# A hybrid block of delta-rule attention, SSD and two quantised FFNs: the last level of a block inverse done by 64x64 quarters, one decay read from an exponential, and a new instruction order

## The chip, the cores and the metric

The kernel runs on one core of a Trainium2 chip. The metric is the device time of one execution in microseconds; lower is better. Every run below is of the same inputs.

## The reference

A batch of 32 sequences of 256 tokens, 128 features each, goes through four residual layers: gated delta-rule attention, a feed-forward layer with int32 weights scaled by 1/127, an SSD (state-space) layer, and the same feed-forward layer again. Each begins with a layer norm.

```python
x = x + attn(_layernorm(x))   # below
x = x + ffn(_layernorm(x))    # silu(x wg^T) * (x wu^T), then wd^T; 128 -> 384 -> 128
x = x + ssd(_layernorm(x))
x = x + ffn(_layernorm(x))
```

The attention keeps a 128x128 state per sequence and updates it token by token:

```python
def step(S, ins):
    q_t, k_t, v_t, a_t, b_t, g_t = ins
    kkT = k_t[:, :, None] * k_t[:, None, :]
    trans = a_t[:, :, None] * (I - b_t[:, :, None] * kkT)
    vkT = v_t[:, :, None] * k_t[:, None, :]
    S = jnp.einsum('bij,bjk->bik', S, trans) + b_t[:, :, None] * vkT
    o = jnp.einsum('bc,bcd->bd', q_t, S) * g_t
    return (S, o)
```

The SSD layer projects to z, x, B, C and dt, applies a causal convolution of 4 taps and a silu to x, B and C, and computes a decayed, causal sum over the tokens with 4 heads of 64 channels. With `dA = dt * A` and its running sum `cs`, the weight of token j in the output of token i is `(C_i . B_j) * exp(cs_i - cs_j) * dt_j`, for j up to i. Then come a gate by silu(z), an RMS norm and an output projection.

## The kernel before

**Units and tiles.** Two sequences, 512 tokens, make a unit; there are 16 units. A unit's activations are NT = 4 tiles of 128 tokens by 128 features, kept as one 128 x 512 tile. Everything is float32, save for the three bfloat16 pieces that some SSD sums are cut into. A float32 matmul is two passes of TensorE, a transpose one.

**Attention as chunks.** A sequence is two chunks of 128 tokens. Inside a chunk the recurrence is a triangular system: with `neg` (lines 726 to 740) holding the negative decayed products of the keys (`diag` is its four diagonal 128x128 blocks), the kernel needs the inverse of (I - diag) of each. It is built in two stages.
- The 16x16 blocks on the diagonal, by substitution. Eight DMAs (`blocks`, line 748) write the blocks to DRAM and eight more (`rows`, 757) read them back, each broadcast over its 16 partitions. Then 15 pairs of small VectorE instructions, `step` and `u` (764 to 771), make the inverses of all blocks at once, and one GpSimd multiply (`x`, 774) sets them on the diagonal of the 128 x 512 tile `x`.
- Three levels (`LEVELS` = 16, 32, 64; lines 781 to 795) merge pairs of blocks of size d into blocks of 2d. For each of the four tiles: transpose x (`pt`), copy to SBUF (`t`, ScalarE), multiply by `diag` (`p1`), copy (`pm`, ScalarE), multiply by x (`p3`). Then one VectorE `copy_predicated` of 128 x 512 puts those parts of `p3` into `x` that a mask of this level, `m_d`, names. The inverse serves the rest of attention (`wq`, `z`, `po`, `py`).

**SSD.** `pz` gives z and dt, a short chain on VectorE turns dt into `dt` and GpSimd into `dA`. From `dA` come two things. First, `pe`: a matmul with the constant `gt` (ones where the row's token comes after the column's) sums what remains to the end of the first chunk, and one with `le` sums what has passed in the second; `ee` is the exponential of both, `f0 = dt * ee[:, 0]` on GpSimd, and `xe = x * f0` weighs the first chunk's tokens for the sum that goes on to the second chunk (`pf`). Secondly, `cs` (a matmul with 32 columns of weights, `grid`): its sums are cut into three bfloat16 pieces (`cut`), go through DRAM in six DMAs (`cuts`, `sums_s`, `sums_t`) and come back in two row layouts, from which one matmul, `pl`, gives the exponents of all pairs of tokens of a tile. The exponential is taken in place in PSUM; times C.B it is `sm`, and `sy` are four matmuls with it.

**The planner.** No instruction is issued where the code stands. Every call records an operation in a `Planner` (from line 140), with an engine, a modelled busy time, a modelled `late` (what passes after the engine is free until the result can be used) and what it depends on. `run` then goes through the recorded operations as a list scheduler and emits one fixed order per engine: PE (TensorE), VectorE, ScalarE, GpSimd and SP (SyncE, which issues the DMAs). An operation's key is the due time of its unit (`at`: unit number x `period`, with the last units drawn together by `LAST`), plus the distance from the longest chain, plus an offset `STAGE` for its layer. `HOP` is the cost of passing to another engine, `SLACK` the cost of reusing a buffer, `SWITCH` the price put on a change of ScalarE's table, `EARLY` how soon a PSUM bank may be taken before it is needed, `window` how many units may be open. The model's DMA takes 450 ns on SP and its `late` after that, however many are under way. At run time each engine goes through its list strictly in order and waits by semaphores.

**Lines.** As all operations are recorded, the profile gives one line for each kind: L211 is every matmul, L221 every transpose, L231 every activation and L229 every copy on ScalarE, L245 every VectorE instruction, L262 GpSimd, L270 the DMAs. Tiles are told apart by their names, with a letter for the layer: `_a` attention, `_f` and `_h` the two feed-forward layers, `_s` SSD. `p_a` is both `p1` and `p3`, `pt_a` the transposes of the levels, `sm_s`, `sy_ps_s` and `pf_s` those of SSD, `pd_a` the transposes of the decays, with 4 columns of result partitions.

Of the kernel before, what the change touches and what calls it, by code (L numbers as in the profile page):

```python
# [12 lines left out]
BF16 = mybir.dt.bfloat16  # L13
# [4 lines left out]
P = 128  # L18
SEQS = 2
# [126 lines left out]
class Planner:  # L146
# [4 lines left out]
    SLOTS = {"ps": 8, "m": 56, "l": 10, "t": 12, "s": 64, "d": 6, "g": 6, "b": 3, "e": 4}  # L151
    SWITCH = 38400.0
    HOP, SLACK = 100.0, 0.0
    STAGE = (100.0, 0.0, 1700.0, 4100.0)
    EARLY = 2800.0
    SPARE = {"ps": 0.5, "m": 3, "l": 0.5, "t": 1, "s": 2, "d": 0.5, "g": 0.5, "b": 0.5, "e": 0.5}
    LAST = 0.29
    HALF = "be"
    SIZES = {"ps": 512, "m": 512, "l": 1024, "t": 64, "s": 32, "d": 512, "g": 8192, "b": 384, "e": 12288}

# [16 lines left out]
    def add(self, eng, busy, late, emit, outs, ins, table=None, after=(), lock=False):  # L177
        op = Op()
        op.eng, op.busy, op.late, op.emit, op.table, op.lock = eng, busy, late, emit, table, lock
        op.unit, op.n, op.stage = self.unit, len(self.ops), self.stage  # L180
        op.preds, op.succs, op.bufs = {p.n: p for p in after}, [], []
        for v, write in [(v, False) for v in ins] + [(v, True) for v in outs]:
# [35 lines left out]

    def transpose(self, out, in_, ident):
        def emit():  # L220
            self.tc.nc.tensor.transpose(real(out), real(in_), real(ident))  # L221

        self.add("PE", 109, 165, emit, [out], [in_, ident])

# [41 lines left out]

    def dma(self, out, in_, late=3500, queue="SP"):
        def emit():
            engine = self.tc.nc.sync if queue == "SP" else self.tc.nc.scalar
            engine.dma_start(out=real(out), in_=real(in_))  # L270

        self.add(queue, 450, late, emit, [out], [in_])

# [22 lines left out]
    def run(self):  # L296
# [18 lines left out]
        free = dict.fromkeys(engines, 0.0)  # L315
        lock = 0.0
        cands = {e: [] for e in engines}
        slots = {k: [[0.0, i] for i in range(n)] for k, n in self.SLOTS.items()}
# [5 lines left out]
        while len(order) < len(ops):  # L324
            best = None
            for e in engines:
                rest = []
                for op in cands[e]:
                    if op.unit > oldest + self.window:
                        continue  # L330
                    t = max(free[e], op.ready, lock if op.lock else 0.0)
                    ok = True
                    for b in op.bufs:
# [77 lines left out]
def hybrid_block(ctx: ExitStack, tc: tile.TileContext, ins: dict, out: bass.AP):  # L411
# [68 lines left out]
    mask_x = []  # L480
    for d in LEVELS:
        nb = P // (2 * d)
# [150 lines left out]
    def attention(g, x):  # L633
# [26 lines left out]
        copy(row_sb.part(first), pd.part(first))  # L660
        pl.dma(row[0, :].rearrange("(j p) -> j p", p=P), row_sb.part(first), late=3000)
        dec = big([P, SEQS, 2 * P], f"dec_{n}")
        pl.dma(dec.rearrange("p s t -> p (s t)"), row.via(lambda r: r[0, :].partition_broadcast(P)), late=6000)

# [81 lines left out]
        for b in range(NBLK):  # L746
            at = slice(b * BLOCK, (b + 1) * BLOCK)
            pl.dma(
                blocks[0, :].rearrange("(b t j i) -> b j t i", b=NBLK, t=NT, i=BLOCK)[b, :, :, :],
                diag[:, :, at].part(at), late=5000,  # L750
            )
        rows_n = pl.buf("l", [P, NT, BLOCK, BLOCK], f"rows_{n}")
        spread = rows_n.rearrange("p t j i -> p (t j i)")
        for b in range(NBLK):
# [4 lines left out]
                blocks[0, b * size : (b + 1) * size].via(lambda ap: ap.partition_broadcast(BLOCK)),  # L759
                late=6000,  # L760
            )
# [18 lines left out]

        for lv, d in enumerate(LEVELS):
            pt = bank([P, NT, P], f"pt_{n}_{d}")
# [74 lines left out]
    def ssd(g, x):  # L857
# [55 lines left out]
        for i in range(3):  # L913
            pl.dma(
                rows_d[0, :].rearrange("(q i j t) -> i q j t", i=3, j=NT, t=P)[i, :, :, :],
                cut[:, i, :], late=3500,
            )
        s_rows, t_rows = sums_s[g % 2], sums_t[g % 2]
        pl.dma(
            s_rows.part(slice(0, parts)).rearrange("p j t -> p (j t)"),  # L920
            rows_d[0, :].rearrange("(k t) -> k t", t=TOK), late=4000,
        )
        for o in range(2):
            pl.dma(
                t_rows.part(slice(parts + 3 * o, parts + 3 * o + 3)).rearrange("p h j t -> p h (j t)"),
                rows_d[0, :].rearrange("(o h i t) -> o i h t", o=2, h=NH, i=3)[o, :, :, :], late=4000,
            )
# [22 lines left out]
        for s in range(SEQS):  # L950
# [24 lines left out]
            for c in range(2):  # L975
# [97 lines left out]
```

## Time and profile before

| What | us |
|---|---|
| Three runs | 884.88, 884.69, 880.66 |
| Median | 884.69 |
| The profiled execution | 883.38 |
| Its span, first to last instruction | 881.7 |
| PE busy from 200 to 800 us of the span | 594.5 of 600 |
| VectorE busy in that stretch | 485.9 |
| ScalarE busy in that stretch | 441.8 |
| GpSimd busy in that stretch | 218.6 |
| DMA: bytes over the span | 25.3 MB, 29 GB/s |

The profile's engines are PE (TensorE's matmuls), PEld (its weight loads, which overlap PE), DVE (VectorE), ACT (ScalarE), POOL (GpSimd) and SP (the DMA issues). A row of a group reads: line, engine, operation, output tile <- input tiles, shape, count | busy time in us, mean duration in ns | idle time of the engine just before those instructions, and what ended most of it. The slices are 40 equal parts of the span, each digit a tenth of the slice; PEclk is the clock that TensorE was granted, in tenths of full speed. Matmuls are pipelined, so their mean duration is a latency, and several overlap.

### The profile page before, as it was taken

The page shows a single profiled execution, that of the slowest core. Times are in us where ns is not written, and L with a number is a line of the kernel's source. Part 1 is how long each engine was busy: PE and PEld are TensorE (multiplying, and loading weights), DVE is VectorE, ACT ScalarE, POOL GpSimd, SP SyncE. Part 2 cuts the span into 40 slices and gives each one's busy share as a digit, 9 for nine tenths or more (in the row PEclk, how much of TensorE's full clock was granted, in tenths as well). Part 3 has the DMA queues.
Part 4 walks back from the last instruction along what each step waited for, and adds up shares of the span by engine and source line. Part 5 has one row for each costly group of instructions (what it writes and reads, how often), then busy time and mean ns, then how long its engine had stood idle before and what let it go on. Part 6 is the DMA issues. An engine that isn't in the chain of part 4 may idle for free.

```text
span 881.7 us, 15941 instructions
## 1 busy us (share of the span) xinstructions
PE 841.8 (95%) x5145; PEld 654.9 (74%) x5145; DVE 696.4 (79%) x2298; ACT 620.5 (70%) x1385; POOL 347.5 (39%) x581
## 2 busy tenths in 40 slices
PE   4967999999999999999999999999999999999997
PEld 3646877778777788777778877778788787585785
DVE  5676599987989889787988879789967647779972
ACT  4842568584977868685876868588685674789862
POOL 7992234342433525252442535234432022142630
PEclk9987999999999999999999999999999999999999
DMA  6220110001101020110102011011110000000001
GB/s 156 64 73 2 38 26 26 21 1 27 40 25 38 4 54 14 30 37 27 40 1 54 13 29 38 27 41 27 36 30 17 1 1 17 0 13 4 20 1 37
DMA packets 42147, 25.34 MB, mean 29 GB/s; under 512 B 18448, under 2 KB 37840, under 8 KB 42064
## 3 DMA queue, kind: packets, MB, share of 16 engines
q1 hardware_dynamic: 40768, 24.00, 10.5%
q8 instruction: 41, 0.67, 0.3%
q10 hardware_dynamic: 1296, 0.33, 0.2%
q14 instruction: 42, 0.34, 0.1%
HBM read 19.16 MB, written 5.14 MB: 28 GB/s over the span
## 4 chain that ended last, share of the span: by engine, by line
PE 78%; DVE 10%; ACT 6%; POOL 3%; DMA 1%; issue 1%; DVEq 0%; ACTq 0%; SPq 0%
PE p_a L211 9%; PE sy_ps_s L211 6%; PE pc_s L211 5%; PE fg_f L211 5%; PE fu_f L211 5%; PE fy_f L211 4%; PE fg_h L211 4%; PE fu_h L211 4%; PE fy_h L211 4%; PE so_s L211 3%; PE pt_a L221 2%; PE pz_s L211 2%; PE wq_a L211 2%; PE po_a L211 2%; ACT L231 2%; DVE cy_s L245 2%
## 5 line engine op out<-in xcount | busy, mean ns | idle before, releaser
L245 DVE SCALAR_TENSOR_TENSOR cy_s<-pc_s,cw,cy_s 128x510 f32<-128x510 f32 (+2 forms) x192 | 134.2, 734 | 1.4 <-ACT cy_s L231 1.0
L231 ACT ACT_TABLE_LOAD x72 | 92.4, 1283 | 8.9 <-DMA bab<-in_L_attn_a_bb_dram 7.6
L211 PEld LDWEIGHTS fy_h<-wdT,hT_h 128*128 128x128 f32 x384 | 61.8, 191 | 24.5 <-issue 22.5
L211 PE MATMUL fy_f<-wdT,hT_f 128*128 128x128 f32 x384 | 73.7, 275 | 0.0
L211 PEld LDWEIGHTS fy_f<-wdT,hT_f 128*128 128x128 f32 x384 | 61.1, 191 | 13.5 <-issue 12.4
L211 PE MATMUL fy_h<-wdT,hT_h 128*128 128x128 f32 x384 | 68.9, 275 | 0.0
L245 DVE TENSOR_TENSOR step_a<-rows_a,u_a 128x60 f32<-128x60 f32 (+14 forms) x240 | 59.4, 247 | 5.8 <-issue 1.5
L211 PE MATMUL pc_s<-xT_s,w_xbc 128*128 128x512 f32 x128 | 63.8, 596 | 0.1
L245 DVE TENSOR_TENSOR u_a<-u_a,step_a 128x60 f32<-128x60 f32 (+14 forms) x240 | 58.8, 245 | 4.0
L211 PE MATMUL sy_ps_s<-xd_s,sm_s 128*128 128x64 f32 x512 | 60.4, 273 | 1.0 <-DVE sm_s L245 1.0
L211 PEld LDWEIGHTS sy_ps_s<-xd_s,sm_s 128*128 128x128 f32 x512 | 59.3, 192 | 1.6 <-DVE sm_s L245 1.2
L231 ACT ACTIVATE cy_s<-pc_s,cb,cw 128x512 f32<-128x512 f32 x64 | 48.3, 774 | 13.3 <-PE pc_s L211 13.1
L211 PEld LDWEIGHTS p_a<-t_a,neg_a 128*128 128x128 f32 x384 | 50.0, 198 | 8.3 <-issue 4.3
L211 PE MATMUL p_a<-t_a,neg_a 128*128 128x128 f32 x384 | 54.3, 284 | 1.4 <-ACT t_a L229 1.4
L262 POOL TENSOR_TENSOR sy_s<-sy_s,yo_s 128x256 f32<-128x256 f32 x32 | 23.6, 756 | 81.0 <-DVE yo_s L245 67.8
L245 DVE COPY_PREDICATED x_a<-m,p_a 128x512 f32<-128x512 int32 x48 | 34.9, 728 | 25.6 <-PE p_a L211 25.4
L211 PE MATMUL p_a<-x_a,pm_a 128*128 128x128 f32 x384 | 54.0, 279 | 0.9 <-ACT pm_a L229 0.9
L211 PEld LDWEIGHTS p_a<-x_a,pm_a 128*128 128x128 f32 x384 | 50.2, 194 | 4.9 <-ACT pm_a L229 1.8
L229 ACT COPY pm_a<-p_a 128x512 f32<-128x512 f32 x48 | 28.1, 584 | 35.3 <-PE p_a L211 35.2
L211 PE MATMUL fg_h<-xT_h,wgT 128*128 128x512 f32 x96 | 48.9, 599 | 0.9 <-ACT fth_h L231 0.6
L245 DVE TENSOR_TENSOR hT_f<-fth_f,fu_f 128x512 f32<-128x512 f32 x48 | 32.8, 683 | 20.8 <-PE fu_f L211 17.9
L211 PE MATMUL fu_f<-xT_f,wuT 128*128 128x512 f32 x96 | 48.6, 592 | 0.0
(214 smaller groups left out, 2364.5 us busy)
## 6 DMA issues: line engine op xcount, KB each, us to landing
rows_a<-blocks_a SPq DMA_DIRECT2D x128, 64.0 KB
x<-in_L_attn_a_x_dram SPq DMA_DIRECT2D x16, 256.0 KB
dec_a<-row_a SPq DMA_DIRECT2D x16, 256.0 KB
out_dram<-x SPq DMA_DIRECT2D x16, 256.0 KB
blocks_a<-neg_a SPq DMA_DIRECT2D x128, 4.0 KB
cuts_s<-cut_s SPq DMA_DIRECT2D x48, 8.0 KB
sums_t<-cuts_s SPq DMA_DIRECT2D x32, 12.0 KB
sums_s<-cuts_s SPq DMA_DIRECT2D x16, 24.0 KB
```

The source lines that it names most:

```text
L211: self.tc.nc.tensor.matmul(real(out), lhsT=real(lhsT), rhs=real(rhs), start=start, stop=stop)
L221: self.tc.nc.tensor.transpose(real(out), real(in_), real(ident))
L229: self.tc.nc.scalar.copy(real(out), real(in_))
L231: self.tc.nc.scalar.activation(real(out), real(in_), func, bias=real(bias), scale=real(scale), **kw)
L245: getattr(self.tc.nc.vector, name)(real(out), *map(real, args), **{k: real(v) for k, v in kw.items()})
L262: getattr(self.tc.nc.gpsimd, name)(real(out), *map(real, args), **{k: real(v) for k, v in kw.items()})
```

## The change

It has three parts.

**The last level by quarters.** When the two 64x64 blocks on the diagonal of x are inverted, only the upper right 64x64 quarter of each tile is still to be found. The loop runs over `LEVELS[:-1]`, and the level d = 64 is written out with `lo` = 0 to 63 and `hi` = 64 to 127: four transposes of the upper left quarter (64x64), a ScalarE copy `t` of 64 x 256, four matmuls `p1` of 64x64 whose result lies in partitions 64 to 127, a copy `pm` of 64 x 256, four matmuls `p3` of 64x64 whose result lies in partitions 0 to 63, and a ScalarE copy of it into x. VectorE's `copy_predicated` of this level and the mask `m_64` go.

**The decay to a chunk's end.** `gt` and its matmul go. The last column of the exponential `ps` of the first chunk already holds the decay from each token to the chunk's end, so `f0` is now a VectorE multiply of 128 x 4 that reads it from PSUM, once per sequence (two per unit), and `xe` follows it. `ee` keeps its second half only.

**The order.** The planner's model of a DMA gets a transfer time (bytes / `RATE`, at least 150 ns), transfers that pass one after the other, and at most `LANES` = 8 in flight; the `late` values are smaller; and the constants of the list scheduler are others. The list of operations is not touched by this, only their order on each engine. `transpose` gets a modelled cost.

```diff
@@ Planner
-    SWITCH = 38400.0
-    HOP, SLACK = 100.0, 0.0
-    STAGE = (100.0, 0.0, 1700.0, 4100.0)
-    EARLY = 2800.0
+    SWITCH = 22500.0
+    HOP, SLACK = 50.0, 110.0
+    STAGE = (-700.0, -600.0, 24500.0, -12600.0)
+    EARLY = 1800.0
-    LAST = 0.29
+    LAST = 0.15
+    RATE = 270.0
+    LANES = 8
...
-    def transpose(self, out, in_, ident):
+    def transpose(self, out, in_, ident, cost=109):
...
-    def dma(self, out, in_, late=3500, queue="SP"):
+    def dma(self, out, in_, late=2300, queue="SP"):
...
-        self.add(queue, 450, late, emit, [out], [in_])
+        v = out if isinstance(out, View) and out.buf.kind not in "dge" else in_
+        half = v.buf.kind in self.HALF or v.buf.dtype == BF16
+        size = (v.lanes[1] - v.lanes[0]) * _count(v) * (2 if half else 4)
+        moves = max(150.0, size / self.RATE)
+        op = self.add(queue, 450, late + moves - 450, emit, [out], [in_])
+        op.moves, op.first = moves, late
@@ Planner.run
+                    if op.moves and len(landed) >= self.LANES:
+                        t = max(t, landed[-self.LANES])
...
+            if op.moves:
+                moved = max(moved, t + op.first - 900) + op.moves
+                op.done = moved + 900
+                landed.append(op.done)
@@ hybrid_block
-    pl = Planner(tc, pools, period=16400.0, window=6)
+    pl = Planner(tc, pools, period=28300.0, window=6)
...
-    le, gt = pl.const([P, P], "le"), pl.const([P, P], "gt")
+    le = pl.const([P, P], "le")
...
-    pool("memset", gt, 1.0)
-    select(gt, ALU.is_gt, 0, [[-1, P]], 1)
...
-    for d in LEVELS:
+    for d in LEVELS[:-1]:
@@ attention: late of the DMAs row 3000 -> 1100, dec 6000 -> 2400, blocks 5000 -> 1400, rows 6000 -> 2100
...
-        for lv, d in enumerate(LEVELS):
+        for lv, d in enumerate(LEVELS[:-1]):
...
+        d = LEVELS[-1]
+        lo, hi = slice(0, d), slice(d, P)
+        pt = bank([P, NT, d], f"pt_{n}_{d}").part(lo)
+        for j in range(NT):
+            pl.transpose(pt[:, j, :], xi_f[:, j, lo].part(lo), ident[:, lo].part(lo), cost=58)
+        t = big([P, NT, d], f"t_{n}_{d}").part(lo)
+        copy(t, pt)
+        p1 = bank([P, NT, d], f"p1_{n}_{d}").part(hi)
+        for j in range(NT):
+            matmul(p1[:, j, :], diag[:, j, hi].part(lo), t[:, j, :], True, True)
+        pm = big([P, NT, d], f"pm_{n}_{d}").part(hi)
+        copy(pm, p1)
+        p3 = bank([P, NT, d], f"p3_{n}_{d}").part(lo)
+        for j in range(NT):
+            matmul(p3[:, j, :], pm[:, j, :], xi_f[:, j, hi].part(hi), True, True)
+        copy(xi_f[:, :, hi].part(lo), p3)
@@ ssd: late of the DMAs cuts 3500 -> 1700, sums 4000 -> 1600
-        pe = bank([P, 2, SEQS, NH], f"pe_{n}")
-        matmul(pe[:, 0], gt, dA[:, 0::2, :], True, True)
-        matmul(pe[:, 1], le, dA[:, 1::2, :], True, True)
-        ee = small_([P, 2, SEQS, NH], f"ee_{n}")
+        pe = bank([P, SEQS, NH], f"pe_{n}")
+        matmul(pe, le, dA[:, 1::2, :], True, True)
+        ee = small_([P, SEQS, NH], f"ee_{n}")
         act(ee, pe, AF.Exp)
         f0 = small_([P, SEQS, NH], f"f0_{n}")
-        pool("tensor_tensor", f0, dt[:, 0::2, :], ee[:, 0], ALU.mult, cost=285)
...
-            pool("tensor_tensor", xe, xt[:, 0], f0[:, s, :, None].to_broadcast([P, NH, HD]), ALU.mult)
...
                 act(ps, ps, AF.Exp)
+                if c == 0:
+                    vec("tensor_tensor", f0[:, s, :], dt[:, j, :], ps[:, :, P - 1], ALU.mult)
+                    pool("tensor_tensor", xe, xt[:, 0], f0[:, s, :, None].to_broadcast([P, NH, HD]), ALU.mult)
...
-            vec("tensor_tensor", yo, pf, ee[:, 1, s, :, None].to_broadcast([P, NH, HD]), ALU.mult)
+            vec("tensor_tensor", yo, pf, ee[:, s, :, None].to_broadcast([P, NH, HD]), ALU.mult)
```

More of the change, by code (lines that the diff above doesn't have):

```diff
@@ L181, in add @@
         op.preds, op.succs, op.bufs = {p.n: p for p in after}, [], []
+        op.moves = 0.0
         for v, write in [(v, False) for v in ins] + [(v, True) for v in outs]:
@@ L217, in matmul @@
         self.add("PE", busy, 165, emit, [out], [lhsT, rhs], after=after)
-    def transpose(self, out, in_, ident):
+    def transpose(self, out, in_, ident, cost=109):
         def emit():
             self.tc.nc.tensor.transpose(real(out), real(in_), real(ident))
-        self.add("PE", 109, 165, emit, [out], [in_, ident])
+        self.add("PE", cost, 165, emit, [out], [in_, ident])
     def act(self, out, in_, func, bias=0.0, scale=1.0, accum=None):
@@ L316, in run @@
         lock = 0.0
+        moved, landed = 0.0, []
         cands = {e: [] for e in engines}
@@ L660, in attention @@
         copy(row_sb.part(first), pd.part(first))
-        pl.dma(row[0, :].rearrange("(j p) -> j p", p=P), row_sb.part(first), late=3000)
+        pl.dma(row[0, :].rearrange("(j p) -> j p", p=P), row_sb.part(first), late=1100)
         dec = big([P, SEQS, 2 * P], f"dec_{n}")
-        pl.dma(dec.rearrange("p s t -> p (s t)"), row.via(lambda r: r[0, :].partition_broadcast(P)), late=6000)
+        pl.dma(dec.rearrange("p s t -> p (s t)"), row.via(lambda r: r[0, :].partition_broadcast(P)), late=2400)
         sq = big([P, NT, P], f"sq_{n}")
@@ L749, in attention @@
                 blocks[0, :].rearrange("(b t j i) -> b j t i", b=NBLK, t=NT, i=BLOCK)[b, :, :, :],
-                diag[:, :, at].part(at), late=5000,
+                diag[:, :, at].part(at), late=1400,
             )
@@ L759, in attention @@
                 blocks[0, b * size : (b + 1) * size].via(lambda ap: ap.partition_broadcast(BLOCK)),
-                late=6000,
+                late=2100,
             )
@@ L915, in ssd @@
                 rows_d[0, :].rearrange("(q i j t) -> i q j t", i=3, j=NT, t=P)[i, :, :, :],
-                cut[:, i, :], late=3500,
+                cut[:, i, :], late=1700,
             )
@@ L920, in ssd @@
             s_rows.part(slice(0, parts)).rearrange("p j t -> p (j t)"),
-            rows_d[0, :].rearrange("(k t) -> k t", t=TOK), late=4000,
+            rows_d[0, :].rearrange("(k t) -> k t", t=TOK), late=1600,
         )
@@ L925, in ssd @@
                 t_rows.part(slice(parts + 3 * o, parts + 3 * o + 3)).rearrange("p h j t -> p h (j t)"),
-                rows_d[0, :].rearrange("(o h i t) -> o i h t", o=2, h=NH, i=3)[o, :, :, :], late=4000,
+                rows_d[0, :].rearrange("(o h i t) -> o i h t", o=2, h=NH, i=3)[o, :, :, :], late=1600,
             )
```

## The prediction

> **What bounds the kernel.** I read the page's busy shares, slices and chain of waits first, then the busy time by stage, then the groups of instructions by shape, and at last single instructions on the timeline.
>
> ```profile
> PE 841.8 (95%) x5145; PEld 654.9 (74%) x5145; DVE 696.4 (79%) x2298; ACT 620.5 (70%) x1385; POOL 347.5 (39%) x581
> PE   4967999999999999999999999999999999999997
> PEclk9987999999999999999999999999999999999999
> PE 78%; DVE 10%; ACT 6%; POOL 3%; DMA 1%; issue 1%; DVEq 0%; ACTq 0%; SPq 0%
> ```
>
> TensorE is busy 95% of the span and carries 78% of the chain that ended last. The four weak slices at the left are its start, where the granted clock dips too. The stages tell it in numbers (columns: window, its length, then busy time of PE, PEld, DVE, ACT, POOL with counts, then clock, DMA share, GB/s):
>
> ```profile
> 0.00:22.00 22.00, 9.92 (x44) 7.33 (x45) 12.26 (x70) 10.24 (x28) 15.96 (x48) 1.00 0.61 157
> 44.00:66.00 22.00, 14.95 (x52) 8.87 (x52) 16.84 (x43) 9.97 (x24) 20.91 (x35) 0.84 0.27 72
> 66.00:88.00 22.00, 16.75 (x95) 14.49 (x95) 15.21 (x58) 6.15 (x12) 4.58 (x6) 0.77 0.01 4
> 200.00:800.00 600.00, 594.52 (x3709) 466.85 (x3707) 485.89 (x1602) 441.79 (x973) 218.59 (x353) 1.00 0.10 25
> 860.00:882.00 22.00, 17.17 (x87) 11.36 (x85) 6.36 (x10) 5.70 (x11) 1.01 (x1) 0.97 0.13 37
> ```
>
> From 200 to 800 us PE idles 5.5 us in 600: there only less PE work can shorten the time, and DVE (486 of 600) and ACT (442) are worth nothing by themselves. Before 88 us PE idles about 25 us, with POOL full from 44 to 66 us (20.91 of 22); at the end it idles some 5 us. So the change is priced as PE work taken away, idle time at the start, and waits that a new order may put into the 99% full middle.
>
> ```profile
> L211 PE MATMUL p_a<-t_a,neg_a 128*128 128x128 f32 x384 | 54.3, 284 | 1.4 <-ACT t_a L229 1.4
> L211 PE MATMUL p_a<-x_a,pm_a 128*128 128x128 f32 x384 | 54.0, 279 | 0.9 <-ACT pm_a L229 0.9
> L221 PE MATMUL pt_a<-ident,x_a 128*128 128x128 f32 x192 | 31.9, 280 | 3.7 <-DVE x_a L245 3.7
> L211 PE MATMUL pe_s<-dA_s,gt 128*128 128x8 f32 x32 | 4.6, 216 | 0.0
> L245 DVE COPY_PREDICATED x_a<-m,p_a 128x512 f32<-128x512 int32 x48 | 34.9, 728 | 25.6 <-PE p_a L211 25.4
> L229 ACT COPY w_a<-wq_a 128x256 f32<-128x256 f32 x16 | 6.0, 372 | 29.9 <-PE wq_a L211 29.8 <-DVE pr_a L245 0.2
> ```
>
> The mean of a matmul (284 ns) is latency; what it takes from PE is the distance to the next start. In the trace a float32 matmul is two passes, each 430 ns for 512 columns, 217 for 256 and 112 for 128; a 128-column transpose is one pass of 109.
>
> **Part 1, the last level by quarters: PE.** Two 128x128 matmul groups of four per unit become two groups of four of 64x64: 16 units x 8 x 2 = 256 passes of 112 ns, 28.7 us. No 64-column pass of this form is in the trace; from 430, 217 and 112 I estimate 57 ns, 14.6 us. That would save 14.1 us, if a 64x64 matmul sits in the queue like any other. The only float32 matmuls here that don't use the whole array suggest that it doesn't: `cs_s`, a tile 32 columns wide (PE rows, then a PEld row):
>
> ```profile
> 168.49 0.39 PE L211 MATMUL fy_f<-wdT,hT_f 128*128 128x128 f32 x2
> 168.81 0.41 PE L211 MATMUL cs_s<-le,grid_s 128*32 128x128 f32 x2
> 169.14 0.71 PE L211 MATMUL so_s<-w_out,gT_s 128*128 128x128 f32 x4
> 169.14 0.52 PEld L211 LDWEIGHTS so_s<-w_out,gT_s 128*128 128x128 f32 x4 [0.20 <-issue]
> ```
>
> The second `fy_f` pass starts at 168.60, `cs_s` at 168.81 (205 ns later where 112 is usual); its second pass starts at 168.94, the next weights load only at 169.14 after 0.20 us of idle for which no releaser is shown, and that matmul 107 ns later (308 ns from the `cs_s` pass, where I would expect 57 for a 64-column pass). All 16 visits look the same. A visit to another tile size so costs 93 + 251 = 344 ns beyond the passes. In the new PE order the 64x64 matmuls come in 18 + 19 visits (a few groups are split by full-size work): 37 x 0.344 = 12.7 us. Net -1.4 us; ends -14.1 (no visit cost) and -1.4.
>
> The transposes: 64 of 109 ns become 64 of about 58: -3.3 us. Do they pay the visit? The nearest row is the transpose `pd_a`, also into a narrow tile (4 columns): its neighbours stand 109 ns away on both sides, no gap. I take -3.3; with the gap, 21 visits x 0.344 = 7.2, it is +3.9.
>
> [...]
>
> **Part 1, elsewhere.** DVE loses 16 x 728 ns = 11.6 us of copies; ACT gains 16 copies of 128x256 or less (372 ns, 6.0 us) and its 32 other copies shrink from 583 to about 372 (-6.8). Both ends lie behind PE, so I cost them at 0. One level's chain of hops also shortens by 0.2 + 0.2 + 0.35 us; PE work covers it in the middle.
>
> **Part 2, decay from the exponentials.** Sixteen matmuls against `gt` go. The two of `pe_s` in a unit start 142 ns apart in all (31 + 111): 16 x 0.142 = -2.3 us of PE. POOL loses 16 x 204 ns; DVE gains 32 multiplies of 128x4, by the row `z_s` (152 ns) 4.9 us; the net DVE change is -6.8 us. `f_s` was ready early and now waits for the cuts, two DMA trips (7 us measured from the last cut to `pl`) and the exponential; behind that DVE multiply queues `sm_s`, which needs the same exponential anyway, and behind `xe` on POOL (614 ns) queues y's last addition. `pf` waits for `xe` 0.15 + 0.61 us after the exponential, and has `sy` matmuls (8 x 224 ns) between: 0. Without that cover it is 32 x 0.77 = 25 us, which is why I looked at the order: PE has 2.5 us of work from `pl` to `sy` and 3 to 5 from `pf` on.
>
> **Part 3, the order.** The instruction order is fixed in the program, so I added the PE work (by the distances above) that stands between an instruction and the one that depends on it.
> - From `kk1` to the first transpose of the same unit: 57 us in mid-run before, 26 to 27 after. That stretch has to hold `neg`, 16 SP transfers (7.3 us of issue, their landing 2), 30 small DVE steps, and `x_a` on POOL (1.29 us). Before it took 30.0 (first unit), 38 (middle), 26.2 us (last). DVE has 22.4 to 26.0 us of work placed there after, plus 1.6 for `x_a` and hops: 24.0 to 27.6 against 26.5. Mean excess I take as 0.2 us, x 16 = +3; ends 0 and 1 us x 16 = +16.
> - Cuts to `pl`: 25 before, 7 to 10 after, need 7. Hops within a level: 2.6 to 3.5 before, 0.9 to 1.1 after, need 0.84 (163 ns of matmul, 30, the 585 ns copy, 60). Covered: 0; if not, 144 hops x 0.1 = 14, the same size as the loop's bad end.
> - Start: in the first unit the transpose `pt_16` came at 63.7 us with 36.4 us of PE work ahead; after, 25.4. From it to `pt_64` took 14.1 us with 4.9 of work inside; after, 11.0 inside. If `x_a` came at the same time, PE would lose 11.0 - 6.1 = 4.9 us; if it comes e earlier, 4.9 - e. POOL, full to 62 us, has about 10 us less ahead of that `x_a` (fewer later units' front work, no `gt` or `m_64` masks), and DVE's steps waited 3.7 us behind POOL's casts. I take e = 8: -3 us; ends e = 13 (all of both) -8, and e = 0 +5.
> - Table loads on ACT 72 to 66 (1283 ns each): -7.7 us, behind PE, 0. SP has 436 transfers as before. The end: 16.6 us of PE work instead of 19.0 follow the last unit's `so`, a chain of hops bounds it: 0.
>
> **Sum.** PE work -1.4 - 3.3 - 2.3 = -7.0; start -3; loop +3. The profiled execution took 883.4 us (span 881.7), 1.3 below the median 884.7: 883.4 - 7.0 = 876.4. I forecast 876.
>
> **Rivals.**
> - A, *every visit drains, transposes too, and the order gives nothing*: -1.4 + 3.9 - 2.3 = +0.2, so 883.6. For it: `cs_s`, 16 of 16. Against: `pd_a`.
> - B, *no visit cost*: a 64x64 matmul with its own row group is not a 32-column tile. -14.1 - 3.3 - 2.3 - 3 + 3 = -19.7, so 863.7. Against: the only row that exists.
> - C, *the DVE loop becomes the bound*: place, the DVE queue between `neg` and `x_a`; price, about 1 us per unit and 16 us in all; it decides once that stretch takes over 26.5 us. -7.0 - 3 + 16 = +6, so 889.4. For it: 38 us measured in the middle before, though DVE had other work in that time; and DVE already bounds 800 to 840 us. Against: DVE is 79% busy and gets 6.8 us less.
>
> **Numbers.** 0.5% (4.4 us) is about what a measurement of this kernel can tell from no change: faster is below 880.3, slower above 889.1. Chances: the forecast 0.45 (own range 869 to 881), A 0.20 (880 to 886), B 0.13, C 0.22 (886 to 895). The forecast gives 0.43 to faster and 0.02 to same; A 0.18 same, 0.02 faster; B all faster; C 0.02 same and 0.20 slower. Together 0.58, 0.22, 0.20. The range from B's side (861) to C's middle (890) holds 8 in 10.
>
> **What would show it.** Passes of 64x64 near 57 ns and a gap of 0.2 us at both ends of a group say part 1 is right; gaps around `pt` say A, none at all B. The middle's windows should keep PE over 98.5% busy; idle before `pt_16` with `x_a` or DVE steps as releaser says C. The unit-0 `pt_16` should start near 56 us. `pf` waiting on `xe`, or `pl` on the sums, would break part 2's zero. The prediction is wrong if PE busy time does not fall by about 7 us, or if idle in 200 to 800 us exceeds 10.

## The result and the profile after

The changed kernel takes 897.71 us (median of 4 runs, 895.58 to 899.65), against 884.4 for the kernel before in the same job: a ratio of 1.0136, 95% interval 1.0095 to 1.0178. It is slower by 13 us, where 8 us faster was forecast; the range ended at 890. The profiled execution took 899.65 us and has a span of 897.8 us, 16.1 more than before; it lies 2 us above the median, the one before 1 us below it.

The page's busy shares, slices, clock and chain of waits of the changed kernel:

```profile
PE 856.1 (95%) x5113; PEld 646.8 (72%) x5113; DVE 669.4 (75%) x2314; ACT 606.8 (68%) x1395; POOL 349.6 (39%) x559
PE   5689999999999999999999999999999999899897
PEclk9889999999999999999999999999999999989689
PE 69%; ACT 10%; DVE 10%; POOL 5%; issue 2%; DMA 2%; SPq 2%; DVEq 0%; ACTq 0%; POOLq 0%
```

DVE and ACT are busy for 27 and 14 us less (7 and 8.5 were counted; of DVE's, 11.6 are the copies and 17.7 the small steps `step` and `u`, which are as many as before but took less time each, 209 and 210 ns on the mean for 247 and 245; the decay's new multiplies add 4.8), but PE is busy for 14 us *more* with fewer instructions: busy time here also holds passes at a lowered clock and the changes of tile size (13.1 us behind 740 us and 17.4 us in all, worked out below). The second new thing is on the right: the clock falls to 0.6 in a slice near 840 us, where before it was full. By stages (window, length, then busy PE, PEld, DVE, ACT, POOL, clock, DMA share, GB/s), first the kernel before, then the changed one, each from 740 us to its end:

```profile
740.00:881.70 141.70, 133.33 (x769) 97.51 (x767) 103.69 (x303) 99.21 (x208) 45.52 (x73) 1.00 0.05 14
```

```profile
44.00:66.00 22.00, 20.52 (x104) 14.62 (x103) 19.24 (x68) 15.06 (x45) 18.19 (x32) 0.86 0.15 44
66.00:88.00 22.00, 20.36 (x147) 16.41 (x145) 17.55 (x67) 11.69 (x33) 8.88 (x13) 1.00 0.21 51
200.00:800.00 600.00, 589.85 (x3616) 448.53 (x3615) 451.90 (x1561) 420.83 (x956) 212.00 (x328) 0.99 0.09 24
740.00:897.80 157.80, 143.97 (x739) 106.23 (x737) 105.59 (x315) 97.01 (x207) 45.58 (x68) 0.91 0.04 11
```

The start is better filled (20.5 and 20.4 us of PE in windows that had 15.0 and 16.8). But from 740 us on the changed kernel needs 157.8 us where the old one needed 141.7, with fewer PE instructions left (739 against 769).

Busy time misleads here, so I counted starts: each PE pass at its full-speed length (430, 217, 112, 109 ns as in the prediction, 57 or 58 for 64 columns) is *work*; what passes beyond it until the next start is *loss*, be it a wait, a change of tile size or a lowered clock; the time before the first pass and after the last counts as loss too. The two profiled executions then differ so:

| us | before | after | difference |
|---|---|---|---|
| PE work | 811.9 | 792.3 | -19.6 |
| Loss up to 132 us | 41.9 | 37.2 | -4.7 |
| Loss from 132 to 740 us | 14.1 | 33.6 | +19.5 |
| Loss from 740 us to the end | 13.8 | 34.7 | +20.9 |
| Span | 881.7 | 897.8 | +16.1 |

**The middle** is above all the price of the 64x64 tiles. One visit on the PE timeline of the changed kernel (start, length, then the group):

```profile
373.15 0.94 PE L214 MATMUL sy_ps_s<-xd_s,sm_s 128*128 128x64 f32 x7
374.03 0.68 PE L214 MATMUL p_a<-x_a,pm_a 64*64 64x64 f32 x8
374.63 0.77 PE L214 MATMUL sy_ps_s<-xd_s,sm_s 128*128 128x64 f32 x5
```

The seventh `sy` pass starts at 373.82 (112 ns apart), the first 64x64 pass only 205 ns later; they follow each other at 58 ns, the first after 106; the last starts at 374.48, the next `sy` 148 ns later (58 would do) and the one after that 160 (112 would do). Over the visits that have no wait beside them a matmul visit loses 318 ns (36 of 37) and a transpose visit 269 ns (19 of 21). That is 11.8 + 5.6 = 17.4 us, of which 13.2 (27 and 17 visits) fall into the middle; the other 6 there are scattered waits for copies and activations of ScalarE. The groups' rows show the same passes without it:

```profile
L214 PE MATMUL p_a<-x_a,pm_a 64*64 64x64 f32 x128 | 11.4, 225 | 0.0
L214 PE MATMUL p_a<-t_a,neg_a 64*64 64x64 f32 x128 | 11.2, 225 | 0.1
L224 PE MATMUL pt_a<-ident,x_a 64*64 64x64 f32 x64 | 7.5, 224 | 1.5 <-DVE u_a L248 1.5
L224 PE MATMUL pd_a<-ident,ab_a 128*4 128x128 f32 x16 | 4.4, 273 | 0.1
```

No column says what a visit costs: "idle before" is nearly zero, since the gap is counted to nobody.

**The end** is waits and the clock. The longest wait, on the timeline of the changed kernel:

```profile
781.44 1.28 ACT L234 ACT_TABLE_LOAD   x1
781.45 1.03 PE L214 MATMUL pl_s<-sums_t,sums_s 93*128 93x512 bf16 x4
782.86 2.03 ACT L234 ACTIVATE pl_s<-pl_s 128x512 f32<-128x512 f32 x4
784.01 0.73 DVE L248 SCALAR_TENSOR_TENSOR cy_s<-pc_s,cw,cy_s 128x508 f32<-128x508 f32 x1
784.73 0.68 DVE L248 SCALAR_TENSOR_TENSOR sm_s<-pl_s,cb_s 128x512 f32<-128x512 f32 x1
785.55 0.63 PE L214 MATMUL sy_ps_s<-xd_s,sm_s 128*128 128x64 f32 x4 [3.07 <-POOL xe_s L265]
```

`sy` of unit 12 stands in PE's order right behind `pl`. It has to wait for a table load, the exponential and `sm`, which queues behind a convolution step on DVE. (The row names POOL's `xe`, but the first `sm` ends at 785.41, 0.14 us before `sy` starts.) The next work in PE's list is `sy` itself, so PE stands. The windows after it:

```profile
780.00:790.00 10.00, 6.93 (x43) 5.65 (x43) 9.16 (x20) 8.73 (x20) 6.09 (x8) 0.88 0.01 2
790.00:800.00 10.00, 9.86 (x48) 8.24 (x48) 7.47 (x26) 6.20 (x17) 2.62 (x6) 0.78 0.00 0
830.00:840.00 10.00, 7.70 (x40) 6.20 (x38) 8.22 (x18) 9.16 (x20) 6.37 (x9) 0.77 0.04 9
840.00:850.00 10.00, 10.00 (x48) 9.64 (x49) 4.23 (x15) 1.24 (x3) 2.33 (x3) 0.55 0.00 0
```

A window with PE 7 to 8 us busy is followed by one with PE full and a mean clock of 0.78 or 0.55: part of the passes run at half speed (from 835.41 to 849.06 us the granted clock is 0.50, and 128-column passes start 213 ns apart where 112 is usual). Behind 740 us the half clock costs 13.1 us (before: none).

### The profile page after: what moved, and what is told of

Its sections match the earlier page's. It is cut to its first block, busy times and chain, and to the rows that moved or that the text cites. A ratio compares the mean times of both kernels' runs of the same rounds, so it can differ in the third digit from the quotient of the medians.

```text
span 897.8 us, 15836 instructions
## 1 busy us (share of the span) xinstructions
PE 856.1 (95%) x5113; PEld 646.8 (72%) x5113; DVE 669.4 (75%) x2314; ACT 606.8 (68%) x1395; POOL 349.6 (39%) x559
## 4 chain that ended last, share of the span: by engine, by line
PE 69%; ACT 10%; DVE 10%; POOL 5%; issue 2%; DMA 2%; SPq 2%; DVEq 0%; ACTq 0%; POOLq 0%
PE p_a L214 7%; PE sy_ps_s L214 5%; PE fu_h L214 4%; PE fy_f L214 4%; PE fy_h L214 4%; PE fg_h L214 4%; PE fu_f L214 4%; PE pc_s L214 3%; PE fg_f L214 3%; PE so_s L214 2%; PE wq_a L214 2%; ACT L234 2%; PE po_a L214 2%; PE pt_a L224 2%; PE pf_s L214 2%
## 5 line engine op out<-in xcount | busy, mean ns | idle before, releaser
L248 DVE TENSOR_TENSOR step_a<-rows_a,u_a 128x4 f32<-128x4 f32 (+14 forms) x240 | 49.5, 209 | 20.7 <-DMA rows_a<-blocks_a 9.0
L232 ACT COPY t_a<-pt_a 128x512 f32<-128x512 f32 (+1 forms) x48 | 24.4, 512 | 56.7 <-PE pt_a L224 56.5
L234 ACT ACTIVATE cy_s<-pc_s,cb,cw 128x512 f32<-128x512 f32 x64 | 48.5, 780 | 17.7 <-PE pc_s L214 17.6
L265 POOL TENSOR_TENSOR x_a<-u_a,blk 128x512 f32<-128x512 f32 x16 | 20.4, 1274 | 91.8 <-DVE u_a L248 36.5
L248 DVE TENSOR_TENSOR u_a<-u_a,step_a 128x4 f32<-128x4 f32 (+14 forms) x240 | 49.7, 210 | 3.5
L214 PEld LDWEIGHTS p_a<-t_a,neg_a 128*128 128x128 f32 (+1 forms) x384 | 42.1, 172 | 11.6 <-ACT t_a L232 4.0
L265 POOL TENSOR_TENSOR xd_s<-xt_s,dt_s 128x512 f32<-128x512 f32 x32 | 32.9, 1043 | 43.5 <-ACT xt_s L232 38.4
L214 PEld LDWEIGHTS p_a<-x_a,pm_a 128*128 128x128 f32 (+1 forms) x384 | 41.8, 172 | 9.7 <-ACT pm_a L232 4.4
L214 PE MATMUL p_a<-t_a,neg_a 128*128 128x128 f32 (+1 forms) x384 | 48.4, 260 | 0.1
L214 PE MATMUL fg_f<-xT_f,wgT 128*128 128x512 f32 x96 | 47.7, 600 | 0.9 <-ACT fth_f L234 0.9
L214 PE MATMUL p_a<-x_a,pm_a 128*128 128x128 f32 (+1 forms) x384 | 48.0, 261 | 0.3 <-ACT pm_a L232 0.3
```

Of the source, the lines that this page charges most:

```text
L214: self.tc.nc.tensor.matmul(real(out), lhsT=real(lhsT), rhs=real(rhs), start=start, stop=stop)
L232: self.tc.nc.scalar.copy(real(out), real(in_))
L234: self.tc.nc.scalar.activation(real(out), real(in_), func, bias=real(bias), scale=real(scale), **kw)
L248: getattr(self.tc.nc.vector, name)(real(out), *map(real, args), **{k: real(v) for k, v in kw.items()})
L265: getattr(self.tc.nc.gpsimd, name)(real(out), *map(real, args), **{k: real(v) for k, v in kw.items()})
```

## The experiments

Sixteen kernels. The old planner's constants are called the old order; "due times" are STAGE, period and LAST; "model" is the DMA model with HOP, SLACK, SWITCH and EARLY. Loss is counted as above, in the profiled execution; the end is its last 141.7 us (the length that was left behind 740 us before), half clock that in the end. One execution stands for each kernel there, and it can lie above the median: e10's took 890.3 us, e5's 900.7, e13's 890.0.

| Kernel | us | Ratio (interval) | Work | Start | Middle | End | Half clock |
|---|---|---|---|---|---|---|---|
| before | 884.4 | 1 | 811.9 | 41.9 | 14.1 | 13.8 | 0 |
| after | 897.7 | 1.0136 (1.0095-1.0178) | 792.3 | 37.2 | 33.7 | 34.6 | 13.1 |
| e1 edits, old order | 894.1 | 1.0106 (1.0064-1.0147) | 792.3 | 41.9 | 38.4 | 19.3 | 3.3 |
| e2 old operations, new order | 914.8 | 1.0368 (1.0309-1.0426) | 811.9 | 37.2 | 31.1 | 32.2 | 5.9 |
| e3 after, old due times | 882.5 | 0.9982 (0.9962-1.0002) | 792.3 | 37.9 | 26.9 | 22.4 | 6.7 |
| e4 after, old LAST | 910.6 | one run | 792.3 | 37.5 | 39.8 | 39.4 | 10.3 |
| e5 after, whole transposes | 897.0 | 1.0117 (1.0082-1.0153) | 795.5 | 37.0 | 30.4 | 36.1 | 14.9 |
| e6 after, extra matmuls | 894.4 | 1.0095 (1.0062-1.0127) | 797.0 | 36.8 | 35.3 | 22.3 | 1.5 |
| e7 after, whole last level | 904.6 | 1.0195 (1.0159-1.0232) | 809.6 | 33.0 | 24.4 | 36.1 | 14.8 |
| e8 after, old STAGE | 923.2 | 1.0476 (1.0404-1.0549) | 792.3 | 39.4 | 62.9 | 27.3 | 8.5 |
| e9 e3, whole transposes | 881.4 | 0.9961 (0.9940-0.9982) | 795.5 | 38.5 | 22.9 | 23.6 | 8.0 |
| e10 quarters, old order | 884.3 | 1.0010 (0.9980-1.0040) | 794.5 | 47.7 | 33.0 | 13.4 | 0 |
| e11 decay, old order | 890.9 | 1.0076 (1.0043-1.0110) | 809.6 | 42.0 | 16.2 | 20.9 | 6.2 |
| e12 e9, visits known | 884.0 | 0.9992 (0.9969-1.0014) | 795.5 | 35.9 | 24.8 | 25.2 | 6.2 |
| e13 before, HOP 90 | 886.9 | 1.0033 (1.0013-1.0052) | 811.9 | 39.8 | 16.2 | 20.3 | 4.9 |
| e14 e9, old decay | 884.4 | 0.9989 (0.9974-1.0004) | 797.8 | 37.4 | 26.3 | 21.3 | 4.9 |
| e15 old operations, new model | 884.8 | 0.9980 (0.9959-1.0001) | 811.9 | 36.8 | 14.1 | 22.1 | 6.4 |
| e16 after, other due time at the end | 904.1 | 1.0212 (1.0180-1.0244) | 792.3 | 36.3 | 35.2 | 38.8 | 12.6 |

**Operations or order: e1, e2.** e1 is the changed kernel with the old planner, e2 the old operations with the new planner.

> The changed kernel's operations (quarters, and the decay read from the exponential) put in order by the old planner (old constants, old model of a DMA). Theory 1 (the new order makes it slow, the operations are slightly good): counting starts of PE passes in the two traces, the new operations take 19.6 us less of passes and the 64x64 visits give 15.0 us back, so 4.6 us less PE work: about 880 us, between 876 and 884. Theory 2 (the operations make it slow: visits to 64x64 tiles and xe waiting for the exponential): 892 us or more, whatever the order.

> The old kernel's operations put in order by the new planner (new constants, DMA model with transfer times and eight in flight). Theory 1 (the order makes it slow): 898 + 4.6 = about 902 us, at least 895, with a half-clock stretch behind 760 us. Theory 2 (the operations make it slow): 880 to 886 us.

894.1 and 914.8. e2 is as theory 1 said, and worse. But e1 is theory 2's number: neither the operations nor the order is harmless. The two do not add up either (9.7 + 30.4 against 13.3), so an order is good or bad for one list of operations. Of e1's 24.3 us of added loss in the middle, 12.9 are its 43 visits there and up to 5.1 a stretch of half clock near 158 us.

**Which half of the new order: e3, e4, e15.**

In short:

```diff
 e3:  -STAGE = (-700.0, -600.0, 24500.0, -12600.0), LAST = 0.15, period=28300.0
      +STAGE = (100.0, 0.0, 1700.0, 4100.0), LAST = 0.29, period=16400.0
 e4:  -LAST = 0.15
      +LAST = 0.29
 e15: e2 with the edit of e3
```

> The changed kernel with only the due times taken back: STAGE, period and LAST are the old ones; the DMA model, HOP, SLACK, SWITCH and EARLY stay new. Theory 1a (the due times crowd the SSD layers of the last units together, and the loss lies behind 760 us): 21 us of loss at the end goes, so 876 to 882 us. Theory 1b (the smaller hop and DMA times make the order too tight everywhere): still over 892 us.

> The changed kernel with LAST alone back from 0.15 to 0.29. If the drawing together of the last units is the cause of the loss behind 760 us: 880 to 886 us. If it is STAGE with its spread of 37 us between the SSD and the second feed-forward layer: 893 us or more.

> The operations of the kernel before, with the new DMA model, HOP, SLACK, SWITCH and EARLY, and the old due times (STAGE, period, LAST). The cell that is missing: old operations took 884.5 with the old planner and 914.8 with the whole new one. Theory 1 (the due times carry the loss of the new order, for the old operations too): 880 to 890. Theory 2 (the new model and hops are bad for the old operations): 900 or more.

With the due times taken back the changed operations fall from 897.7 to 882.5, the old ones from 914.8 to 884.8. So the due times lose 15 and 30 us, and the model with its hops is harmless (884.8 against 884.4 for the old operations). LAST alone is not it: e4 is at 910.6. e3 loses 12 us less than the changed kernel at the end and 7 less in the middle; it is still above the old kernel's end (22.4 against 13.8). With the old operations the due times cost more in the middle than at the end: from e2 to e15 17 us of loss go in the middle and 10 at the end.

**What the quarters are worth: e5, e7, e10.** e5 and e7 keep the order of every engine as it is in the changed kernel and only widen the tiles; the copies between them, left out here, follow (whole tiles in e7).

```diff
 e5:
-pl.transpose(pt[:, j, :], xi_f[:, j, lo].part(lo), ident[:, lo].part(lo), cost=58)
+pl.transpose(pt[:, j, :], xi_f[:, j, :], ident, cost=58)
...
 e7, also:
-matmul(p1[:, j, :], diag[:, j, hi].part(lo), t[:, j, :], True, True)
+matmul(p1[:, j, :], diag[:, j, :], t[:, j, :], True, True, cost=2 * (2 * d / 2.4 + 4.5))
...
-matmul(p3[:, j, :], pm[:, j, :], xi_f[:, j, hi].part(hi), True, True)
+matmul(p3[:, j, :], pm[:, j, :], xi_f[:, j, :], True, True, cost=2 * (2 * d / 2.4 + 4.5))
```

> The changed kernel with the same instruction order on every engine, but the last level's transposes are of whole 128x128 tiles again (the copy still takes the 64x64 quarter); matmuls stay 64x64. Theory 1 (a 64x64 transpose pays the change of tile size like a matmul: 0.27 us a visit in the trace of the changed kernel, 21 visits, 5.7 us, against 64 x 0.051 = 3.3 us of passes saved): 2.4 us faster than the changed kernel, about 895.3. Theory 2, the prediction's (transposes pay nothing, by the row of the decay's transpose): 3.3 us slower, about 901.

> The changed kernel in the same order, with the whole last level on 128x128 tiles again (transposes, both matmul groups and their two copies of 128x512); only the last copy takes the quarter. Theory 1 (the changes of tile size give back what the quarters save: 19.6 - 2.3 = 17.3 us of passes against 37 x 0.32 + 21 x 0.27 = 17.5 us): within 2 us of the changed kernel, 896 to 900, a little more if the longer copies show. Theory 2 (the quarters are worth what their passes say): 910 us or more.

> The kernel before with the quarters alone (old planner, old decay path). The two parts together took 894.1 in the old order, 9.6 over the kernel before. Theory 1 (the old constants fit the old operations, and any edit shuffles the order; which edit does not matter): this one and the next both come out over 884.4, by 3 to 12 us. Theory 2 (one edit carries it: the decay's, whose xe and f_s wait for the exponential and hold up the queues): this one 880 to 884, the decay alone 892 or more.

e5 (897.0) and the changed kernel (897.7) can't be told apart: 3.2 us more work, 3.3 less loss in the middle. So the transposes pay the visit, by the timeline. The time alone says it less clearly, since e5's six executions run from 891 to 901 us, and 901 was forecast if they paid nothing. The same edit in the order of e3 settles it: e9 was expected at about 880 us if they pay and at 886 if not, and took 881.4 (12 executions, 879.6 to 883.6; e3 882.5). e7, between its two theories, adds 17.3 us of passes and gets 13.5 back in start and middle (4.2 + 9.3); its time rises by 6.9. So of 17.3 us of saved passes the quarters are worth 4 to 7 in this order, and nothing in the old order (e10, 884.3). In e10's profiled execution (890.3 us) the middle loses 18.9 us more than the old kernel's (33.0 against 14.1), for 17.4 of work saved: 12.1 are the 40 visits there at the prices above, and nearly all of the rest is a stretch of 13.7 us at half clock near 163 us. Its start is 5.8 us worse, of which up to 3.4 is half clock.

**The decay: e11, e14.** The parts one by one: e11 is the old kernel with only the decay read from the exponential, e14 is e9 with the old decay.

> The kernel before with the decay from the exponentials alone (old planner, whole last level). Theory 1: 887 to 896, like the quarters alone. Theory 2 (the decay's waits carry the loss): 892 or more, with f_s or xe named as releaser of PE's waits, and the quarters alone at 880 to 884.

> The kernel of e9 with the decay's old path (the gt matmul, f0 on GpSimd from ee). Theory 1 (the decay from the exponentials costs, as in the old order: 6.4 us there): 2 to 8 us faster than e9's 881.4, though TensorE has 2.3 us more to do. Theory 2 (in this order it is covered and saves its 2.3 us): 883 to 885.

In the old order the decay costs 6.4 us though PE has 2.3 less to do; the loss is at the end (20.9 against 13.8, 6.2 of it half clock, none before). The longest waits there are for DVE's convolutions (2.6 us) and of `pf` for `xe` (1.7; the kernel before has 1.2). In the order of e9 the same edit comes with 3.0 us less (884.4 to 881.4), but the two intervals overlap, and moving HOP alone is worth 2.4 us (e13). So no price of its own shows: what it costs differs from order to order.

**The clock: e6.** In short:

```diff
+FILL = {"sy_ps_s12_0": 7, "gT_ps_s13_1": 2, "sy_ps_s15_0": 2}
+for _ in range(FILL.pop(name of the op's tile, 0)):
+    nc.tensor.matmul(flat[:, :256], lhsT=w_zd[:, :128], rhs=w_zd[:, :256], start=True, stop=True)
```

> The changed kernel in the same order, with 11 extra matmuls of 128x256 (0.43 us each at full clock) put on TensorE right ahead of three places at the end where it waits: seven ahead of the first sy of unit 12 (idle 3.07 us), two ahead of the second gT of unit 13 (0.96), two ahead of the first sy of unit 15 (1.13). Their results are overwritten. Theory 1 (the clock is halved because TensorE paused; 27 us of half clock there cost 13.1 us): the stretch behind 787 us goes, and with it 3.1 us; if all stretches go, up to 13 us, so 885 to 894. Theory 2 (the half clock comes from elsewhere, or the idle is only one part of it): extra work only, 897 to 899, and the same stretches.

894.4, 3.3 us less with 4.7 us more work (the intervals of the two kernels overlap); in the profiled execution 6.4 less. The intended way failed: the extra matmuls read only a constant (`w_zd`) and still waited, which points to the bank they write, the one that `sy` will use. The PE timeline of e6:

```profile
786.62 4.97 PE L424 MATMUL sy_ps_s<-w_zd 128*128 128x256 f32 x14 [2.99 <-DVE sm_s L249]
```

So the pause is as long as before, and it is DVE's `sm` that ends it, where the changed kernel's line named POOL. Yet the half clock nearly went; windows of e6:

```profile
790.00:800.00 10.00, 9.76 (x66) 8.61 (x64) 6.07 (x18) 3.76 (x8) 1.42 (x2) 0.96 0.00 0
830.00:840.00 10.00, 7.70 (x54) 5.91 (x53) 9.64 (x22) 9.49 (x23) 7.97 (x11) 1.00 0.06 13
840.00:850.00 10.00, 9.26 (x74) 8.20 (x74) 7.61 (x22) 5.58 (x11) 4.89 (x6) 1.00 0.01 2
```

From 830 to 840 us PE is busy for 7.70 us in both kernels; here the clock stays at 1.00. The longest pause there is the same in both:

```profile
834.71 0.66 PE L224 MATMUL gT_ps_s<-ident,gz_s 128*128 128x128 f32 x4 [0.96 <-DVE sm_s L248]
837.42 1.13 PE L424 MATMUL gT_ps_s<-w_zd 128*128 128x256 f32 x4 [0.96 <-DVE sm_s L249]
```

What differs is where it falls. In every one of the eighteen traces the stretches of half clock begin on one grid of 3.413 us. Behind the first 100 us there are 4056 grid windows at full clock (the last 4.5 us left out). All 15 in which PE was busy for less than 41% were followed by half clock, of the 61 between 41 and 71% 23 were, and of the other 3980 none. The grid windows in question, three of the changed kernel, then two of e6:

```profile
784.21:787.62 3.41, 2.07 (x19) 2.10 (x19) 3.41 (x10) 3.03 (x8) 2.19 (x3) 1.00 0.00 0
832.00:835.41 3.41, 1.58 (x8) 0.62 (x6) 3.41 (x9) 3.40 (x11) 3.24 (x5) 1.00 0.06 17
852.47:855.89 3.42, 2.29 (x19) 2.08 (x20) 2.61 (x7) 3.41 (x9) 3.42 (x5) 1.00 0.00 0
784.00:787.41 3.41, 0.79 (x4) 0.72 (x5) 3.41 (x9) 3.41 (x9) 2.45 (x5) 1.00 0.00 0
835.20:838.61 3.41, 1.94 (x8) 1.13 (x8) 3.41 (x9) 3.38 (x12) 3.16 (x6) 1.00 0.08 17
```

All but the last were followed by half clock. In e6 the 0.96 us pause ends 2.2 us into its grid window, in the changed kernel 2.7, and so its window holds 1.94 us of busy PE for 1.58. Both lie between 41 and 71%, and what decides there stays open.

What half clock costs can be read where neither order nor work differs, from the executions of one kernel. Four of e10's have a mean granted clock of 0.992 and took 881.7 to 883.2 us; three have 0.978 to 0.982 and took 889.3 to 890.5. For e5 it runs from 0.986 and 891.1 us to 0.975 and 900.7. The four executions of the changed kernel have 0.978 to 0.982, those of e6 0.987 to 0.990. That half clock costs the changed kernel several us at its end is shown.

**The due times in detail: e8, e16.** e8 takes STAGE back alone, e16 changes the SSD's offset from 24500 to 12000 for the last four units only.

> The changed kernel with the offsets of the layers (STAGE) alone taken back; period 28300 and LAST 0.15 stay. Theory 1 (the SSD's due time, 24.5 us late, puts unit 12's SSD off until nothing is left to run beside it): unit 12's cs comes before 750 us of the span (772.6 in the changed kernel, 742.5 before) and the time is 880 to 888. Theory 2 (the period or LAST crowd the end): it stays behind 760 us and the time above 892.

> The changed kernel with one number different, and for the last four units alone: the SSD's offset in STAGE is 12000 in place of 24500; the order up to the 570th us stays as it was. Theory 1 (the late due time puts unit 12's SSD behind the feed-forward layers of units 13 to 15, so that nothing is left to run beside the last four SSDs): unit 12's cs comes before 755 us of the span (772.6 in the changed kernel), waits and half clock in the last 122 us fall from 23.9 us towards the 4.5 of the kernel before, and the time to 880 to 890. Theory 2 (the loss at the end is the last four SSDs' own chain, wherever they stand): 894 or more.

Theory 1 misses in both, and both come out where theory 2 put them (e8: `cs` of unit 12 at 763.7 us). But e8, the slowest of all (923.2), is no picture of a crowded end: its loss is in the middle (62.9), with five waits of `pf` for `xe` (4.4 us), waits for the convolution's activations, and 49 matmul visits where the changed kernel has 37. STAGE fits its period. In e16 unit 12's `cs` did come at 745.6 instead of 772.6 us, yet the end lost 38.8 us, and units 13 and 14 then came together (806.3 and 808.1). So it is not unit 12's place by itself, and which number of the due times makes the end bad stays open; the three belong together.

**How sturdy an order is, and the visits in the planner: e13, e12.** e13 is the old kernel with HOP 90 for 100. e12 is e9 with a planner that charges 145 ns where PE enters or leaves small tiles and prefers to stay.

> The kernel before with one constant of its planner moved a little: HOP 100 to 90, no operation changed. It measures what a shuffle of the order is worth by itself. Theory 1 (the old constants sit on a narrow good spot): 888 us or more. Theory 2 (the order is sturdy): 882 to 887.

> The kernel of e9 (old due times, whole transposes) whose planner knows the change of tile size: it adds 145 ns where TensorE passes into or out of matmuls with fewer than 128 weight columns and prefers to stay. Theory 1 (changes of tile size are a real cost and split groups can be saved): the 33 or so visits fall to 32, 0.3 us; the steady pitch of a unit stays at 49.5 us; 879 to 882. Theory 2 (what decides is where the order leaves pauses at the end, whatever the visits): anything between 876 and 892, with the difference from e9 in waits and half clock behind 760 us.

886.9, 0.33% slower (interval 0.13 to 0.52): a shuffle of the order by itself moves the end by some us (20.3 against 13.8 of loss there). The old kernel's short end is rare: of all orders here only e10's has one like it (13.4), the others lose 19.3 us or more. e12 has 30 visits for 33, and no gain (884.0 against 881.4 for e9; ratios 0.9992 and 0.9961): what it saves is under what the shuffle moves.

**The best version.** e9, the changed operations with whole transposes in the last level, the new model and the old due times: 881.4 us, ratio 0.9961 (0.9940 to 0.9982). It beats both kernels, the old one by 0.4%, as the lowest of sixteen. From unit 2 to unit 9 `cs` follows every 49.4 us, as in e3 (49.5; old kernel 50.9, changed kernel 50.4); up to unit 11 it is 50.9 (51.0; 51.5, 50.9), so the gain in the middle is small. The end still loses 9.8 us more than the old kernel's. Moving `cs` of unit 13 (3.6 us of wait at 784 us) behind the work that was ready was not tried.

## Why the prediction was wrong

- *What bounds the kernel*: PE, right: by starts, PE work and loss make up the whole span. Both of the prediction's own signs of being wrong came: PE busy time rose by 14.3 us, and PE idles 10.15 us from 200 to 800 us (above 10).
- *Part 1, matmuls*: -1.4, right: 13.8 us of passes saved and 11.8 of visits, -2.0. 344 ns a visit were taken from `cs_s`, 318 measured; 57 ns a pass, 58 measured. `cs_s` was the right neighbour to read it from, though the 308 ns in that sum are not in its rows: they start the next matmul at 169.14, 200 ns behind the `cs_s` pass, and the one after it 213 ns later, which makes 93 + 143 + 101 = 337.
- *Part 1, transposes*: "their neighbours stand 109 ns away on both sides, no gap. I take -3.3". Mis-sized: 3.3 us of passes against 5.6 of visits by the timeline, nothing measurable by e5, against -3.3. The row of `pd_a` was the wrong neighbour: it loads 4 columns of weights over all 128 rows, and its neighbours stand without a gap in the changed kernel too (109 or 110 ns to the next start after 15 of 16). The 64x64 transposes lose 269 ns a visit, so rival A's +3.9, +0.2 for the sum, was nearer.
- *PE work*: -7.0 forecast; 19.6 - 17.4 = 2.2 us less by the timeline, 4 to 7 by e7 for the quarters alone (e7's order has other waits where the visits were).
- *Part 2*: 16 x 0.142 = 2.3 us less PE work, exact (811.9 to 809.6 in e11). The cover, costed at 0, held: `pf` waits for `xe` 0.7 us in the middle of the changed kernel and not at all behind 740 us, where the long wait is that of `sy` for `sm`. In the old order the same edit costs 6.4 us (e11).
- *Part 3, start*: -3 forecast, -4.7 measured, and that with 4.2 us of visits in it, which part 1 had counted: without them (e7, same order) it is -8.9, up to 3.4 of it less half clock. The mechanism was right: `x_a` of the first unit ends at 53.5 us (63.3 before), 9.8 earlier where 8 was taken, and `pt_16` starts at 54.7.
- *Part 3, the loop of the inverse* (the forecast's +3 and rival C): from `neg` to `x_a` the units 8 to 14 take 23.6 to 27.0 us (37.6 to 44.9 before), as estimated, and in the middle PE does not wait for it, so the +3 was not there: the 1.5 us behind `u_a` in the row above is one wait at 66 us. C's time (889) was the nearest of the four, by another mechanism. The 6 us of scattered waits in the middle are mostly for ScalarE, hops that the prediction held to be covered.
- *Part 3, the end*, the step that failed: "16.6 us of PE work instead of 19.0 follow the last unit's `so`, a chain of hops bounds it: 0." I priced what comes behind the last `so` and not the 120 us before it, and the sum had no term for the clock. In the last 120 us the changed kernel has 54 us of SSD and 33 of the second feed-forward on PE and none of the first (before 59, 39 and 8). Loss behind 740 us: +20.9 us, of which 13.1 is half clock and most of the rest waits. That alone turns -8 into +13. That the waits come from too little other PE work beside the SSD chains is argued from these sums and the wait shown above; no run isolates it, and e16, which moved one chain ahead, lost more.

The profiled difference of 16.1 us so adds up: work and visits -2.2, start without visits -8.9, other waits in the middle +6.3, end +20.9. That the new due times carry the loss is shown (e3, e15 against the changed kernel and e2); that they do so mainly at the end is shown for the changed operations alone (12 of the 18 us of loss that the changed kernel has over e3); by which of the three numbers is open. The other 8.6 us at the end remain with the old due times (e3), as they do in nearly every order here.

## What to carry to other kernels

Price a new order by its thin ends as well as by its full middle: add up, per engine, what is left to run beside the last dependent chains, and count a lowered clock behind pauses as a cost of its own (13.1 us at the end here). A smaller tile saves passes only if the visits are few: here 8 passes a visit saved 0.44 us and the visit took 0.32. Constants of a list scheduler fit one list of operations; compare edits under the same order (e5, e7), or the shuffle (0.3% for one harmless constant) hides them.

## What the runs showed of the hardware

- A transpose into a 64x64 tile pays for the change of tile size like a matmul (269 and 318 ns a visit); a transpose that loads 4 columns of weights over 128 rows does not (109 or 110 ns to the next start after 15 of 16).
- After a visit the second full-size pass is late as well: 92 ns of loss at the exit and 76 more at the next start, so a look at the direct neighbours misses a quarter of the price.
- The granted clock falls to 0.50 in stretches of a whole number of 3.41 us (6.8, 10.2, 13.7 in the changed kernel), on a grid of that length; 128-column passes then start 213 ns apart instead of 112. The longest pauses before the three stretches at the end were 3.07, 0.96 and 1.13 us, in grid windows with PE busy for 61, 46 and 67%, so PE was not idle for a whole window before any of them. Behind the first 100 us of the eighteen traces no window above 71% was followed by half clock, every one below 41% was, and in e6 the pause of 0.96 us at the same place, in a window of 57%, was not.
